# First attention: conditioning two batches ahead, and two products of the adapter merge in its place at the end

## The chip, the cores and the metric

The kernel runs on one core of one Trainium2 chip. The metric is the device time of one execution in microseconds (us). Three runs of the kernel before took 1413.83, 1415.15 and 1416.17 us; their median is 1415.15. All data are float32, but for a small mask in bfloat16.

A core has a matrix engine (TensorE, PE in the profile; PEld is its weight load), a vector engine (VectorE, DVE), a scalar engine for activations and copies (ScalarE, ACT), a general engine (GpSimd, POOL) and a sequencer that issues DMAs (SyncE, SP). Each engine works through its own instructions in order. They wait for one another by semaphores.

## The reference

One transformer block on x of 8 batches x 128 rows x 512 columns.

```python
x = x + attn(cond(x, cond_weight[adapter_ids]), wq, wk, wv, wo)     # first attention
x = x + ffn(cond2(x, Wq, Wk, Wv, Wo, ..., k_cache, v_cache, table, seqlens), ffn weights)

# cond:  h[b] = x[b] @ weight[adapter[b]].T            (512 x 512 per batch, gathered by index)
# attn:  q, k, v = h @ wq, h @ wk, h @ wv              (32 heads of 16, 8 key heads)
#        out = softmax(causal(q k^T * scale)) v @ wo
# cond2: attention with norms, rotary positions and a paged cache (32 heads of 128, 8 key heads)
# ffn:   y @ kernel + bias + low-rank deltas, the low-rank matrices mixed by a gate per batch
```

The change lies in the first attention, which takes the first 212 us or so. The second attention and the feed-forward part fill the rest of the span.

## The kernel before

The text of the program sets the order of every engine's instructions (`manual_schedule`), and the framework adds the semaphores. A tile name with `bufs=n` has n buffers used in turn: the tile after the n-th waits until the first one's readers are done.

**The batch pipeline.** The first attention loops over `k` from 0 to 16. A batch `b` has two rounds, `k = 2b` (even) and `k = 2b + 1` (odd), and each round holds half of its heads. A batch passes through these steps:

- `load_x` (L290): a DMA brings x[b] into `xs_b`, four buffers. The DMAs of batches 2 and 3 are issued by POOL, the others by SP.
- `gather_w` (L296): four indirect DMAs of 256 KB, issued by POOL, bring the batch's 512 x 512 conditioning weight into tiles `cw` from a pool of twelve (tag `a`), which is three batches of weights.
- `flip_x` (L497, L503): PE transposes xs into PSUM and ACT copies it out as `xT` (two buffers).
- `condition` (L512, L520): 16 logical products on PE (32 instructions) give `hp`, which ACT copies out as `hT` (four buffers, tag `vg`).
- `project_k`, `project_v` (L543, L550), `project_q` (L528): the projections of hT. `keep_k`, `keep_v`, `keep_q` copy them out on ACT. `keep_v` also has SP store V to memory (`v_kept`, L572) and load it four times, spread over the partitions (`vrep`, L575).
- `scores1` (L593 mask, L605 products), `max1` on DVE (L616), `exps1` on ACT (L636), `divide1` on DVE and POOL (L644 to L646), `turn1`, DVE's transposes (L655), and `values1` on PE (L671).
- `out_proj1` (L693): PE's product; DVE adds xs (L697) and SP stores the sum (`x_kept`, L698). `flip_x1` (L497, L702) transposes it for the second attention.

In the kernel before, round `2b` makes the conditioning of the next batch, and the key projection that reads it follows on PE a little later in the same round. The lines that set this, as PE meets them in an even round:

```python
scores1(k)                  # of batch b
condition(b + 1)            # products, then ACT copies hT
flip_x1(b - 2)
kv = project_k(b + 1)       # reads that hT
values1(b - 1, (1, 0))
project_v(b + 1, kv)
```

The odd round ends with `project_q(b + 1)`, then `flip_x(b + 2)`, and `load_x(b + 4)` on SP's queue. The tile that this load fills is that of batch `b`, which `out_proj1(b)` reads in round `2b + 3`. SP holds the load until then, and what stands behind it in SP's queue too.

**The merge.** The feed-forward part needs low-rank matrices mixed by the gates. `merge_loads` brings them in, `merge_gates` (L441, L447) prepares gate tiles on DVE and POOL, and `merge_a` (L456, L463) makes one of four products on PE with a copy on ACT. All share the pool of twelve tiles with the conditioning weights. The rounds after the last conditioning also issue the first gathers of the second attention's cache (`vg`, `kg`, L160) on POOL.

**PSUM.** Products of conditioning, projections, out_proj1 and merge_a take turns in two buffers (`p_mm`), transposes and values1 in two others (`p_tp`), scores in two more (`p_sc`).

Of the kernel before, what the change touches and what calls it, by code (L numbers as in the profile page):

```python
# [20 lines left out]
B, S, DM = 8, 128, 512  # L21
# [20 lines left out]
def block_kernel(  # L42
# [47 lines left out]
    def tile_a(shape, name):  # L90
        return both.tile(shape, F32, tag="a", name=name, bufs=12)
# [184 lines left out]
    with (  # L276
# [9 lines left out]
        def load_x(b):  # L286
            if b < B:
                xss[b] = p1.tile([P, DM], F32, tag="xs", name=f"xs_{b}", bufs=4)
                queue = nc.gpsimd if b in (2, 3) else nc.sync
                queue.dma_start(out=xss[b][:], in_=x[b])  # L290

        def gather_w(b):
            if b < B:
                cws[b] = [tile_a([P, DM], f"cw_{b}_{c}") for c in range(KC)]
                for c in range(KC):
                    nc.gpsimd.indirect_dma_start(  # L296
                        out=cws[b][c][:],
                        out_offset=None,
                        in_=cond_w,
                        in_offset=bass.IndirectOffsetOnAxis(ap=idx_w[:, c, b : b + 1], axis=0),  # L300
                    )
# [191 lines left out]
        def transposed(src, name):  # L493

            tp = p_tp.tile([P, 4, P], F32, tag="tp", name=name)
            for c in range(4):
                nc.tensor.transpose(tp[:, c, :], src[:, c * P : (c + 1) * P], ident[:])  # L497
            return tp

        def flip_x(b):  # L500
            tp = transposed(xss[b], f"xTp_{b}")
            xT[b] = both.tile([P, KC, S], F32, tag="kg", name=f"xT_{b}", bufs=2)
            nc.scalar.copy(xT[b][:], tp[:])  # L503

        def condition(b):
            hp = p_mm.tile([P, KC, S], F32, tag="mm", name=f"hp_{b}")
            parts = [(oc, c) for oc in range(KC) for c in range(KC)]
            if b == 0:

                parts.sort(key=lambda part: part[1])  # L510
            for n, (oc, c) in enumerate(parts):
                nc.tensor.matmul(  # L512
                    hp[:, oc, :],
                    cws[b][c][:, oc * P : (oc + 1) * P],
                    xT[b][:, c, :],
                    start=(n == 0 if b == 0 else c == 0),
                    stop=(n == KC * KC - 1 if b == 0 else c == KC - 1),
                )
            hT[b] = both.tile([P, KC, S], F32, tag="vg", name=f"hT_{b}", bufs=4)
            nc.scalar.copy(hT[b][:], hp[:])  # L520

        def new_q(b):
            return p_mm.tile([P, REP, S], F32, tag="mm", name=f"qp1_{b}")
# [24 lines left out]
        def project_v(b, ps):  # L548
            for c in range(KC):
                nc.tensor.matmul(  # L550
                    ps[:, 1, :], hT[b][:, c, :], wv_sb[:, c, :], start=(c == 0), stop=(c == KC - 1)
                )
# [76 lines left out]
        def exps1(k, n):  # L629
            h = H[k]  # L630
            b, hb = divmod(k, 2)
            if hb == 0:
                prs[b, n] = p1.tile([P, 2, 8, S], F32, tag=f"pr1_{n}", name=f"pr1_{b}_{n}")
            sc = h["sc"][n][:].rearrange("p j (h t) -> p (j h) t", t=S)
            for m in range(8):
                nc.scalar.activation(  # L636
                    prs[b, n][:, hb, m, :], sc[:, m, :], AF.Exp, bias=h["nm", n][:, m : m + 1]
                )
# [11 lines left out]
        def turn1(k, n):  # L650


            b, hb = divmod(k, 2)
            pr = prs[b, n][:, hb].rearrange("p m t -> p (m t)")
            nc.vector.transpose(pr, pr)  # L655
# [34 lines left out]
        def out_proj1(b):  # L690
            ps = p_mm.tile([P, DM], F32, tag="mm", name=f"att1_{b}")
            for r in range(REP):
                nc.tensor.matmul(  # L693
                    ps[:], oT[b][:, r, :], wo_sb[:, r, :], start=(r == 0), stop=(r == REP - 1)
                )
            x1[b] = p1.tile([P, DM], F32, tag="x1", name=f"x1_{b}", bufs=1)
            nc.vector.tensor_tensor(x1[b][:], ps[:], xss[b][:], ALU.add)  # L697
            nc.sync.dma_start(out=x1_kept[b][:], in_=x1[b][:])  # L698

        def flip_x1(b):  # L700
            tp = transposed(x1[b], f"x1Tp_{b}")
            nc.scalar.copy(x1T[b][:], tp[:])  # L702
# [17 lines left out]
        for k in range(2 * B + 1):  # L720
            b, hb = divmod(k, 2)
            more, now, last = b + 1 < B, k < 2 * B, k - 1
            if now:
                scores1(k)
            if hb == 0:

                for n in range(2):
                    if k:
                        turn1(last, n)
                    if now:  # L730
                        max1(k, n)
                if more:
                    condition(b + 1)
                if k == 2 * B - 2:
                    for i in range(2):
                        merge_a(i, p_mm.tile([P, 512], F32, tag="mm", name=f"aeff_{i}"))
                if b >= 2:
                    flip_x1(b - 2)
                if now:
                    exps1(k, 0)  # L740
                    exps1(k, 1)
                if more:
                    kv = project_k(b + 1)
                if k == 2 * B:
                    t = p_sc.tile([P, 2, 4 * S], F32, tag="sc", name="merged")
                    for i in range(2):
                        merge_b(i, t[:, i, :])
                    queries(0)
                if k:
                    values1(b - 1, (1, 0))  # L750
                if now:
                    divide1(k, 0)
                if more:
                    project_v(b + 1, kv)
                if k == 2 * B - 2:
                    for i in range(2, KC):
                        merge_a(i, p_mm.tile([P, 512], F32, tag="mm", name=f"aeff_{i}"))
                if k == 2 * B:
                    for i in range(2):
                        merge_w(i)  # L760
                if k:
                    values1(b - 1, (3, 2))
                if now:
                    divide1(k, 1)
                if more:
                    keep_k(b + 1, kv)
                    keep_v(b + 1, kv)

                if b:
                    gather_w(b + 3)  # L770
                if b == B - 3:
                    gather(0, "vg")
                elif b == B - 2:
                    gather(0, "kg")
                if k == 2 * B - 4:
                    merge_gates()
            else:
                max1(k, 0)
                max1(k, 1)
                turn1(last, 0)  # L780
                if b >= 1:
                    out_proj1(b - 1)
                exps1(k, 0)
                exps1(k, 1)
                divide1(k, 0)
                divide1(k, 1)
                turn1(last, 1)
                if more:
                    ps = new_q(b + 1)
                    project_q(b + 1, ps, range(REP - 1))  # L790
                else:
                    for c in range(KC):
                        q_matmul(0, c)
                    for part in q_turn(0):
                        part()
                    for c in range(KC):
                        kv_matmul(0, c)
                if more:
                    project_q(b + 1, ps, (REP - 1,))
                    keep_q(b + 1, ps)  # L800
                else:
                    kv_turn(0)
                    norms(0)
                if b + 2 < B:
                    flip_x(b + 2)
                load_x(b + 4)
                if b == 1:
                    tables(0)
                    load_qkv(0)
                    load_wo(0)  # L810
                elif b == 2:
                    tables(1)
                    nc.gpsimd.memset(minus_half[:], -0.5)
                elif b == 3:
                    load_qkv(1)
                if b == 4:
                    indices()
                    nc.sync.dma_start(out=bias[:], in_=ffn_b.unsqueeze(0).to_broadcast([P, DM]))
                    merge_loads()
# [407 lines left out]
```

## Time and profile before

| | us |
|---|---|
| median of three runs | 1415.15 |
| the profiled execution, whole | 1413.75 |
| its span, first to last instruction | 1412.0 |
| PE busy in the span | 1379.3 (98%) |
| DVE, ACT, POOL busy | 931.5, 649.6, 569.9 |
| a steady batch of the first attention (65.8 to 85.8) | 20.0 |
| PE busy in that stretch | 19.76 |

The profile's page gives the busy time of each engine, the granted clock of PE, and the costliest groups of instructions. Answers from its trace give the same for any stretch: instructions in order of time (start, length, engine, line of the program, output and inputs, shape, count), with the idle time before one of them in square brackets and the engine or DMA that ended it. The waits list who waited for whom: total us, number of times, longest. Times are from the start of the span. SPq marks the issue of a DMA by SP, not its transfer. A DMA's landing shows only where an instruction waits for it.

### The profile page before, as it was taken

The page shows a single profiled execution, that of the slowest core. Times are in us where ns is not written, and L with a number is a line of the kernel's source. Part 1 is how long each engine was busy: PE and PEld are TensorE (multiplying, and loading weights), DVE is VectorE, ACT ScalarE, POOL GpSimd, SP SyncE. Part 2 cuts the span into 40 slices and gives each one's busy share as a digit, 9 for nine tenths or more (in the row PEclk, how much of TensorE's full clock was granted, in tenths as well). Part 3 has the DMA queues.
Part 4 walks back from the last instruction along what each step waited for, and adds up shares of the span by engine and source line. Part 5 has one row for each costly group of instructions (what it writes and reads, how often), then busy time and mean ns, then how long its engine had stood idle before and what let it go on. Part 6 is the DMA issues. An engine that isn't in the chain of part 4 may idle for free.

```text
span 1412.0 us, 21833 instructions
## 1 busy us (share of the span) xinstructions
PE 1379.3 (98%) x7012; PEld 889.7 (63%) x7012; DVE 931.5 (66%) x2251; ACT 649.6 (46%) x1515; POOL 569.9 (40%) x557
## 2 busy tenths in 40 slices
PE   6999999999999999999999999999999999999998
PEld 5777755666666666666666666666666565566555
DVE  3878756666666666666666666666666666666651
ACT  3555525444444444444444444444444344344431
POOL 5685633433333333444444343333343433343220
PEclk9999989999999999999999999999999999999999
DMA  7255503444444765444446654444456544444440
GB/s 247 81 160 168 173 31 102 132 119 118 118 119 118 204 180 121 120 120 120 120 120 192 177 136 120 118 120 120 119 165 191 151 111 132 135 111 110 116 112 31
DMA packets 161970, 185.62 MB, mean 131 GB/s; under 512 B 93057, under 2 KB 103553, under 8 KB 161857
## 3 DMA queue, kind: packets, MB, share of 16 engines
q1 hardware_dynamic: 146304, 139.64, 35.5%
q0 software_dynamic: 15552, 44.58, 11.0%
q8 instruction: 57, 0.93, 0.3%
q14 instruction: 57, 0.46, 0.1%
HBM read 80.03 MB, written 5.77 MB: 61 GB/s over the span
## 4 chain that ended last, share of the span: by engine, by line
PE 92%; DVE 2%; ACT 1%; issue 1%; POOL 1%; DMA 1%; SPq 1%; DVEq 0%; POOLq 0%; ACTq 0%
PE op L988 19%; PE qp L177 15%; PE sc L914 15%; PE yp L1007 15%; PE kvp L217 7%; PE sc L921 4%; PE fp L1069 2%; PE qTp L254 2%; PE hp L512 2%; PE o L671 2%; PE att L693 1%; PE qp L528 1%; PE sc L605 1%; ACT pr L636 1%; DMA cw<-in_cond_w_dram,idx_w 1%
## 5 line engine op out<-in xcount | busy, mean ns | idle before, releaser
L927 DVE CUSTOM_DVE_ANT_0 pr<-sc,mask,nq 128x640 f32<-128x640 f32 x256 | 225.9, 884 | 141.1 <-PE sc L921 129.4
L937 ACT ACTIVATE pr<-pr,nm 128x640 f32<-128x640 f32 x256 | 211.8, 827 | 190.0 <-DVE nm L927 187.2
L914 PE MATMUL sc<-kT,qT 128*128 128x512 f32 x512 | 263.3, 596 | 0.0
L177 PE MATMUL qp<-wq,x1T 128*128 128x512 f32 x512 | 251.2, 593 | 0.0
L988 PE MATMUL op<-pT,vg 128*128 128x256 f32 x1024 | 242.0, 379 | 1.4 <-DMA pT<-fl 1.4
L203 POOL TENSOR_TENSOR qa<-qa,qb 128x512 f32<-128x512 f32 x64 | 81.8, 1278 | 376.6 <-DVE sums L904 376.5
L1007 PE MATMUL yp<-wo,oT 128*128 128x512 f32 x504 | 228.6, 596 | 0.0
L988 PEld LDWEIGHTS op<-pT,vg 128*128 128x128 f32 x1024 | 193.9, 190 | 27.7 <-DVE sums L904 1.6
L905 ACT ACTIVATE pr<-pr,sums 128x640 f32<-128x640 f32 x256 | 208.4, 814 | 0.0
L908 DVE STREAM_TRANSPOSE fl<-pr 128x640 f32<-128x640 f32 x252 | 189.2, 808 | 0.0
L921 PEld LDWEIGHTS sc<-kTo,qT 128*128 128x128 f32 x512 | 96.7, 190 | 125.1 <-issue 103.7
L1007 PEld LDWEIGHTS yp<-wo,oT 128*128 128x128 f32 x504 | 91.4, 191 | 92.5 <-issue 91.1
L160 POOL DMA_INDIRECT kg<-in_k_cache_dram,idx_kv x128 | 132.2, 1033 | 35.3 <-issue 35.2
L160 POOL DMA_INDIRECT vg<-in_v_cache_dram,idx_kv x128 | 127.4, 995 | 37.6 <-issue 32.6
L914 PEld LDWEIGHTS sc<-kT,qT 128*128 128x128 f32 x512 | 88.1, 192 | 81.3 <-issue 78.1
L256 ACT COPY qT<-qTp 128x512 f32<-128x512 f32 x64 | 37.5, 586 | 209.5 <-PE qTp L254 206.1
L217 PEld LDWEIGHTS kvp<-wkv,x1T 128*128 128x128 f32 x512 | 97.3, 190 | 40.5 <-issue 30.4
L217 PE MATMUL kvp<-wkv,x1T 128*128 128x256 f32 x512 | 121.0, 379 | 0.0
L244 POOL TENSOR_TENSOR rs<-ss,minus_half 128x5 f32<-128x5 f32 x64 | 76.5, 1196 | 82.6 <-DVE ss L242 81.7
L177 PEld LDWEIGHTS qp<-wq,x1T 128*128 128x128 f32 x512 | 82.9, 191 | 32.0 <-issue 32.0
L921 PE MATMUL sc<-kTo,qT 128*128 128x128 f32 x512 | 99.4, 276 | 0.0
L273 ACT COPY kTo<-kTp 128x128 f32<-128x128 f32 x64 | 17.1, 267 | 163.6 <-PE kTp L271 163.6
(151 smaller groups left out, 1671.2 us busy)
## 6 DMA issues: line engine op xcount, KB each, us to landing
pT<-fl SPq DMA_DIRECT2D x1008, 80.0 KB
kT<-flk SPq DMA_DIRECT2D x480, 32.0 KB
wq<-in_wq_dram SPq DMA_DIRECT2D x8, 1024.0 KB
wo<-in_wo_dram SPq DMA_DIRECT2D x8, 1024.0 KB
vrep<-v_kept SPq DMA_DIRECT2D x32, 128.0 KB
wkv<-in_wkv_dram SPq DMA_DIRECT2D x8, 512.0 KB
vg<-in_v_cache_dram,idx_kv POOLq DMA_INDIRECT x128, 3.7
kg<-in_k_cache_dram,idx_kv POOLq DMA_INDIRECT x128, 3.8
```

Source lines behind the costliest of these rows:

```text
L160: nc.gpsimd.indirect_dma_start(out=dst[:, c].rearrange("p n d -> p (n d)"), out_offset=None, in_=src, in_offset=bass.IndirectOffsetOnAxis( ...
L177: nc.tensor.matmul(s["qp"][:].rearrange("p h d -> p (h d)"), x1T[b][:, c, :], weights[g][0][:, c, :], start=(c == 0), stop=(c == KC - 1),)
L203: nc.gpsimd.tensor_tensor(qa[:], qa[:], qb[:], ALU.add)
L217: nc.tensor.matmul(s["kp"][:], x1T[b][:, c, :], weights[g][1][:, c, :], start=(c == 0), stop=(c == KC - 1))
L905: nc.scalar.activation(prs[r][:], prs[r][:], AF.Copy, scale=sums[:, r : r + 1])
L908: nc.vector.transpose(s["flips"][:, :, :, r, :].rearrange("p b c j -> p c b j"), prs[r][:])
L914: nc.tensor.matmul(sc[:, : NBLK * P].rearrange("p (k j) -> p k j", j=32), s["qT"][:, r, :], s["kT"], start=True, stop=True,)
L921: nc.tensor.matmul(sc[:, NBLK * P : NK], s["qT"][:, r, :], s["kTo"][:], start=True, stop=True)
L927: nc.vector.tensor_tensor_reduce(out=pr[:], in0=sc[:, :NK], in1=mask[:], scale=s["nq"][:, r : r + 1], scalar=3.0e38, op0=ALU.add, op1=ALU.min,
L937: nc.scalar.activation(pr[:], pr[:], AF.Exp, bias=nm[:, r : r + 1], scale=-1.0, accum_out=sums[:, r : r + 1],)
L988: nc.tensor.matmul(ops[h][:, : 2 * S], cached(u, "vg", c) if c < NBLK else s["vo"][:], s["pT"][:, :, c, 2 * h : 2 * h + 2, :].rearrange("p ...
L1007: nc.tensor.matmul(yp[:], s["oT"][:, r, :], weights[g][2][:, r, :], start=(r == 0), stop=(r == REP - 1))
```

## The change

The conditioning of batch b + 2, rather than b + 1, stands in round 2b. Round 0 keeps condition(1), and makes condition(2) as well, with its flip, after project_v. Round 12 has no conditioning left and takes merge_a(0) and merge_a(1) from round 14. The supply moves with it:

- `flip_x(b + 3)` instead of `flip_x(b + 2)` at the end of an odd round.
- `gather_w(4)` in round 1, and `gather_w(b + 4)` instead of `gather_w(b + 3)` in even rounds.
- `load_x(b + 3)` behind `out_proj1(b - 1)` in odd rounds, instead of `load_x(b + 4)` at their end. The same tiles are loaded in the same order.
- `merge_gates` in round 10 instead of round 12.

No instruction is added or removed. The lines after the edited part move down by up to seven.

```diff
@@ -729,9 +729,11 @@
-                if more:
-                    condition(b + 1)
-                if k == 2 * B - 2:
+                if k == 0:
+                    condition(1)
+                elif b + 2 < B:
+                    condition(b + 2)
+                elif b == B - 2:
                     for i in range(2):
                         merge_a(i, p_mm.tile([P, 512], F32, tag="mm", name=f"aeff_{i}"))
@@ -752,6 +754,9 @@
                 if more:
                     project_v(b + 1, kv)
+                if k == 0:
+                    flip_x(2)
+                    condition(2)
@@ -767,12 +772,12 @@
                 if b:
-                    gather_w(b + 3)
+                    gather_w(b + 4)
                 if b == B - 3:
                     gather(0, "vg")
                 elif b == B - 2:
                     gather(0, "kg")
-                if k == 2 * B - 4:
+                if b == B - 3:
                     merge_gates()
@@ -780,11 +785,14 @@
                 if b >= 1:
                     out_proj1(b - 1)
+                    load_x(b + 3)
                 exps1(k, 0)
                 exps1(k, 1)
                 divide1(k, 0)
                 divide1(k, 1)
                 turn1(last, 1)
+                if b == 0:
+                    gather_w(4)
@@ -801,9 +809,8 @@
-                if b + 2 < B:
-                    flip_x(b + 2)
-                load_x(b + 4)
+                if b + 3 < B:
+                    flip_x(b + 3)
```

## The prediction

> **What bounds the kernel now.** I read the page first, then the waits of TensorE (PE) inside the first attention, then the instructions in order of time around each place that the change touches.
>
> ```profile
> span 1412.0 us, 21833 instructions
> PE 1379.3 (98%) x7012; PEld 889.7 (63%) x7012; DVE 931.5 (66%) x2251; ACT 649.6 (46%) x1515; POOL 569.9 (40%) x557
> ```
>
> PE is busy for 98% of the span, so the change can win only idle PE time, and whatever makes PE wait costs its full length. The first attention is the stretch from 25 to 212 us; a steady batch (two rounds k) takes 20.0 us there. Its PE waits (us in total, times, longest):
>
> ```profile
> PE sc L593 <- ACT pr L636: 3.5, 3, 1.8
> PE kvp L543 <- ACT hT L520: 2.6, 7, 0.7
> PE o L671 <- DVE pr L655: 1.3, 2, 1.1
> ```
>
> The second line is what the change aims at: the key projection stands right behind the conditioning whose copy hT it reads. The first is a hole of 3.3 us in round k=0 (PE, then ScalarE (ACT), in order of time: start, us):
>
> ```profile
> 32.14 1.06 PE L550 MATMUL kvp<-wv_sb,hT 128*128 128x128 f32 x8
> 36.70 0.40 PE L593 MATMUL sc<-eye,causal 32*128 32x128 bf16 x14 [1.84 <-ACT pr L636]
> 44.27 0.40 PE L593 MATMUL sc<-eye,causal 32*128 32x128 bf16 x14 [0.27 <-ACT pr L636]
> ...
> 32.40 4.25 ACT L636 ACTIVATE pr<-sc,nm 128x128 f32<-128x128 f32 x16
> ```
>
> PE waits from 33.2 to 36.7 for the sixteen exponentials, because the next scores need their PSUM banks. The end of one odd round (k=3):
>
> ```profile
> 60.74 0.65 DVE L697 TENSOR_TENSOR x<-att,xs 128x512 f32<-128x512 f32 x1
> 61.42 0.35 SPq L290 DMA_DIRECT2D xs<-in_x_dram  x1
> 61.87 0.38 SPq L572 DMA_DIRECT2D v_kept<-vpad  x1
> 63.85 0.60 PE L497 MATMUL xTp<-ident,xs 128*128 128x128 f32 x4
> 66.77 2.10 SPq L575 DMA_DIRECT2D vrep<-v_kept  x4
> ```
>
> The add (L697, ends 61.39) frees an input tile; the load into it leaves at once. The flip at 63.85 reads a tile loaded much earlier. The store v_kept, issued at 61.87, had landed only at 66.77, when its reader could issue: 4.90 us, with the weight gathers (POOL, 59.64 to 64.38) on the same DMA engines. Batch 3 shows 103.16 to 107.59, 4.43 us.
>
> **The change, part by part** (+ is later; all sums are against the profiled execution, 1413.75 us with 1412.0 of span).
>
> *Waits removed.* From round 2 on, project_k reads an hT made one batch earlier. The wait was 0.66 us in round 2, and 0.24 in rounds 4, 6 and 8: -0.66 and -0.72. In round 10 it was 0.24 and a wait for VectorE (DVE) of 0.21 followed it, set by a chain behind L378; a PE that comes later (below) loses both: -0.45. Round 0 keeps its wait, since condition(1) stays there.
>
> *Round 0: flip_x(2) and condition(2).* PE is given four transposes (0.44 us between starts) and 32 products (3.78) in the hole. But the copy xT that condition(2) reads goes into ACT's queue behind the sixteen exponentials, which end at 36.65. So the transposes run in the hole, condition(2) starts at 37.0, and queued behind it on PE is scores1(1), behind that max, exponentials and scores1(2). Here the clock matters (stretches of time: PE busy, its instructions, granted PE clock, DMA):
>
> ```profile
> 13.30:16.70 3.40, 1.53 (x13) 0.99 0.98 367
> 16.70:20.10 3.40, 3.40 (x17) 0.51 1.03 387
> 33.70:37.10 3.40, 0.63 (x20) 1.00 0.02 5
> 37.10:40.50 3.40, 3.40 (x24) 0.50 0.14 43
> ```
>
> Twice a stretch of 3.4 us with little PE work is followed by 3.4 us at half clock. Before, the second of these slowed scores1(1) by 0.5 us and a projection (L528, 4.71 us instead of 3.73) that waited for ACT anyway. After, the same slow stretch falls on condition(2): 3.78 + 1.7 puts its end at 42.5 and scores1(1)'s (1.47) at 44.0, where it was 38.7: **+5.3**. (At full clock +3.8.) kvp_1 now gives its PSUM buffer to project_q(1), after keep_v(1) behind hT_2 on ACT, about 44.05: nothing to speak of. The gathers for batch 2 have landed by then: the DMA share is 0.02 from 33.7 on.
>
> *The loads of x.* load_x(4..7) moves from behind the flip to behind out_proj1, in the round in which flip_x now reads that very tile; SP issues the x1 store first. From the add's end to the flip are 2.46 us (61.39 to 63.85, the same in every batch). The load takes the place in the queue that v_kept had, 0.48 us after the add. Lands at 0.48 + 4.90 + 0.33 (128 KB more ahead of the landing, an estimate from the 387 GB/s of the stretch above), less 2.46: a stall of 3.25 us in round 3; by batch 3's row 2.8 in round 7; between them 3.0 in round 5. In round 9 no weight gather is left beside it: the quiet v_kept (37.41 to 40.52, 3.11) gives 1.46, and the load res late in the kernel (issued 1231.81, read 1234.76, behind a store too) 0.97; I take 1.2. Sum **+10.25**. Behind the flip on PE stand scores1 of the next round and so everything. From below: 4 x 0.97 = 3.9, if gathers don't hinder; from above: 4 x 4.5 = 18, if the vrep loads and large weight loads, now just ahead and behind on SP, queue in as well. No cover is left, as the flip is among the last products of the round.
>
> The Trainium skill weighs in here ("DMA: Bandwidth & Descriptors", Anatomy of one DMA): about 2.0 us fixed plus bytes over 436 GB/s, for the POOL path, which would be 2.6 us for these 256 KB, a stall of 0.6, 2.5 in all. The rows that share the chip's DMA with gathers say 4.4 to 4.9 for half the bytes; I follow the rows.
>
> *The clock after these stalls.* The skill's rule ("TensorE: Matmul & The Clock Gate", HAM oscillation) is to avoid gaps over about 3.4 us; stalls of 3 us would then be free of it, and this part 0. The row at 13.3 speaks otherwise: 1.53 us of work, a gap of 1.9, and half clock followed, while 30.3 to 33.7 with 2.22 of work stayed full. So a stall near 3 us, however it falls across two such stretches, trips the clock about 8 times in 10. One costs 1.35 us, since half of a slow stretch of 3.4, less what falls on idle time, is lost: 3 x 0.8 x 1.35 = **+3.2**; round 9's stall is too short.
>
> *The other moves on the queues.* gather_w goes one batch ahead by taking its first place in round 1 (POOL is free from about 53 to 59) and leaves round 8; there POOL comes earlier, but DVE is held by L378. load_qkv and load_wo are no longer held behind a waiting load on SP and start some 15 us sooner; nothing waited for them. 0.
>
> *The end.* merge_gates moves from round 12 to round 10, merge_a(0, 1) (3.56 us) from 14 to 12, condition(7) out of 12.
>
> ```profile
> 165.59 0.94 POOL L160 DMA_INDIRECT kg<-in_k_cache_dram,idx_kv  x1 [0.30 <-issue]
> 166.56 2.33 POOL L447 TENSOR_TENSOR gs<-gc,sel 128x256 f32<-128x256 f32 x4
> 168.85 3.74 POOL L646 TENSOR_TENSOR pr<-pr,sums 128x1024 f32<-128x1024 f32 x2
> ...
> 167.96 3.72 PE L456 MATMUL aeff<-gs,la 128*128 128x256 f32 x16
> 174.33 1.07 PE L671 MATMUL o<-pr,vrep 32*32 32x128 f32 x40 [1.12 <-DVE pr L655]
> ```
>
> Here POOL sets the time: gathers, gates (2.33), divisions, then DVE's transposes, then o at 174.33. Without the gates o can start 2.29 earlier: -2.29. merge_a no longer fills the time before; PE idles from 168.4 to 172.0. The gates now stand in round 10 behind the vg gathers (to 146.53) and push round 12's transposes to 154.3, where PE wants o at 153.56: +0.79. Together **-1.5**. The idle 3.6 us also drop the clock: **+1.2**. So PE's total work is unchanged, and the emptied slot at the end pays back 2.3, not 3.6.
>
> **Sum:** 5.3 - 0.66 + 10.25 + 3.2 - 0.72 - 0.45 - 1.5 + 1.2 = +16.6. On its own execution 1413.75 gives 1430.4. The median of the runs shown is 1415.15, 1.4 above it: **1431.8 us**, slower. A change of less than 0.2%, 2.8 us, can't be told from none.
>
> **Rivals.**
> *Short stalls, no clock loss (15%).* The loads land as the quiet rows say and stalls stay near 1.2: 5.3 - 0.66 + 4.8 - 2.67 + 1.2 = +8.0, 1423. For it: DMA share in the stretch is under one half on the mean. Against: v_kept's 4.4 and 4.9.
> *Long stalls (11%).* Each near 4.5 us, four clock drops at 1.5: +5.3 - 0.66 + 18 + 6 - 2.67 + 1.2 = +27, 1442. For it: v_kept took 9.2 us beside large weight loads (124.19 to 133.39). Against: those loads now come after.
> *Loads in time, not slower (6%).* The load lands within 1.98 us of its issue, in rounds 3 to 9, and stalls and their clock losses go: 5.3 - 0.66 - 2.67 = +2.0 without a drop at the end, 1417.2, within 0.2%. It decides once the four stalls together are under 0.8 us. Against: no 256 KB load here was used sooner than 2.95 us.
> *The order doesn't do what it says.* PE still waits for hT where the copy is late: 1.8 us less gain. A share of the cases above, no more.
>
> **How the numbers follow.** The likeliest (68%): stalls of 2.3 to 3.6, +12 to +21. The range takes in the short stalls and the lower part of the long ones: 1421.5 to 1440. Outside: loads in time, and most of the long. Faster 0.03 (loads in time and a shorter half-clock stretch after 204 us, whose phase may move by 1.7 us), same 0.05, slower 0.92.
>
> **What would show it.** Right: four waits of the xTp transposes for the xs load, three near 3 us and a last near 1.2; the kvp wait for hT only in round 0; condition(2) starting at 37 under half clock and scores1(1) ending near 44; an idle PE of about 3.6 us before o in round 14. Wrong: no xTp wait for xs, or one under 1 us each; a full clock after the stalls; condition(2) inside the hole.

## The result, and the profile after

The changed kernel takes 1432.02 us (median of six runs, 1424.87 to 1435.46), the kernel before beside it 1414.49 us (six runs, 1412.11 to 1416.17). The ratio is 1.0109, with a 95% interval of 1.0087 to 1.0132: slower by 1.1%. (The ratios in this document are worked out over all runs of both kernels; the quotient of the two medians is near them, 1.0124 here.) The forecast was 1431.8 us and slower. The profiled execution of the changed kernel took 1432.41 us with a span of 1430.6, so the two traces differ by 18.6 us of span, against +16.6 in the sum. The runs also spread more than before, over 10.6 us instead of 4.1.

The page of the changed kernel, the span and the busy time:

```profile
span 1430.6 us, 21837 instructions
PE 1386.5 (97%) x7012; PEld 894.7 (63%) x7012; DVE 931.1 (65%) x2251; ACT 650.2 (45%) x1515; POOL 570.0 (40%) x557
```

PE has the same 7012 instructions and is busy 7.2 us longer (1379.3 before). So of the 18.6 us, 7.2 are the same work done more slowly, and 11.4 are idle PE. The waits of PE from 25 to 230 us of the changed kernel (us in total, times, longest) say where the idle part is:

```profile
PE xTp L497 <- DMA xs<-in_x_dram: 10.1, 4, 3.7
PE hp L512 <- ACT xT L503: 3.5, 1, 3.5
PE o L671 <- DVE pr L655: 2.2, 2, 1.3
PE sc L605 <- issue: 1.4, 2, 1.0
PE sc L593 <- ACT pr L636: 1.2, 1, 1.2
...
PE kvp L543 <- ACT hT L520: 0.7, 1, 0.7
```

The wait for hT went as intended, from 2.6 us in seven to the 0.7 of round 0. Its place is taken by 10.1 us of the flip's transposes waiting for a load. The hole of round 0 stayed: its wait has a new name (condition(2) for xT) and the same length. PE in order of time (start, us, then the instruction, in brackets the wait before it), round 0 first, then the ends of rounds 3, 5, 7 and 9:

```profile
33.17 0.60 PE L497 MATMUL xTp<-ident,xs 128*128 128x128 f32 x4
37.32 5.47 PE L512 MATMUL hp<-xT,cw 128*128 128x128 f32 x32 [3.54 <-ACT xT L503]
42.72 0.40 PE L593 MATMUL sc<-eye,causal 32*128 32x128 bf16 x16
42.95 1.09 PE L605 MATMUL sc<-kbd,qT 32*128 32x256 f32 x16
...
71.92 0.63 PE L497 MATMUL xTp<-ident,xs 128*128 128x128 f32 x4 [3.48 <-DMA xs<-in_x_dram]
72.48 0.40 PE L593 MATMUL sc<-eye,causal 32*128 32x128 bf16 x16
72.71 1.80 PE L605 MATMUL sc<-kbd,qT 32*128 32x256 f32 x16
74.45 4.74 PE L512 MATMUL hp<-xT,cw 128*128 128x128 f32 x32
...
120.04 0.63 PE L497 MATMUL xTp<-ident,xs 128*128 128x128 f32 x4 [2.29 <-DMA xs<-in_x_dram]
...
144.68 0.63 PE L497 MATMUL xTp<-ident,xs 128*128 128x128 f32 x4 [0.64 <-DMA xs<-in_x_dram]
```

Behind the stall at 71.92 the scores take 1.80 us where they take 1.09 in round 0 of this kernel, and the products of the conditioning 4.74 where 3.84 is their usual length. Stretches like this one make up nearly all of the 7.2 us of slower work: over the first 260 us the granted clock costs 15.3 us in this trace and 8.5 in the one before. The granted clock around three of the stalls (stretch of time: its length, PE busy, clock, DMA share, GB/s):

```profile
69.20:72.60 3.40, 0.68 (x12) 1.00 1.00 354
72.60:76.00 3.40, 3.40 (x39) 0.55 1.06 382
93.00:96.60 3.60, 0.02 (x1) 1.00 0.95 350
96.60:100.00 3.40, 3.31 (x37) 0.53 0.00 0
118.00:120.60 2.60, 0.56 (x5) 1.00 1.02 386
120.60:124.00 3.40, 3.40 (x38) 0.52 1.05 385
```

Each stall is followed by about 3.4 us at half clock, the shortest of the three (2.29 us) too. The fourth column of the stall rows points to why the loads are late: the DMA engines are full (0.95 to 1.02) while PE waits. Whose traffic it is that delays them, a run below tests. One of these loads on SP's queue (start, us):

```profile
65.85 0.34 SPq L698 DMA_DIRECT2D x_kept<-x  x1
66.23 0.43 SPq L290 DMA_DIRECT2D xs<-in_x_dram  x1
66.70 0.48 SPq L130 DMA_DIRECT2D wq<-in_wq_dram  x1
```

Issued at 66.23 and read at 71.92: 5.69 us for 256 KB. POOL issues four gathers of conditioning weights at 64.43, 65.73, 66.98 and 68.23, which move 1 MB at the same time. The load of round 9, which has no such gathers beside it, is read 2.98 us after its issue (141.70 to 144.68).

The starts of the key projection and of the second attention's first scores sum it up:

| | before | after | later by | step |
|---|---|---|---|---|
| project_k, round 2 | 50.34 | 54.88 | 4.5 | 4.5 |
| round 4 | 70.35 | 79.45 | 9.1 | 4.6 |
| round 6 | 90.35 | 104.18 | 13.8 | 4.7 |
| round 8 | 111.64 | 127.58 | 15.9 | 2.1 |
| round 10 | 131.64 | 150.61 | 19.0 | 3.0 |
| round 12 | 152.47 | 169.99 | 17.5 | -1.5 |
| scores, second attention | 211.66 | 229.31 | 17.7 | 0.1 |
| end of the span | 1412.0 | 1430.6 | 18.6 | 0.9 |

### The profile page after: what moved, and what is told of

Read it like the earlier page. It is cut to its first block, busy times and chain, and to the rows that moved or that the text cites. A ratio compares the mean times of both kernels' runs of the same rounds, so it can differ in the third digit from the quotient of the medians.

```text
span 1430.6 us, 21837 instructions
## 1 busy us (share of the span) xinstructions
PE 1386.5 (97%) x7012; PEld 894.7 (63%) x7012; DVE 931.1 (65%) x2251; ACT 650.2 (45%) x1515; POOL 570.0 (40%) x557
## 4 chain that ended last, share of the span: by engine, by line
PE 89%; DVE 3%; DMA 2%; issue 2%; POOL 2%; ACT 1%; SPq 1%; POOLq 0%; DVEq 0%; ACTq 0%
PE op L995 19%; PE qp L177 15%; PE sc L921 15%; PE yp L1014 15%; PE kvp L217 7%; PE sc L928 4%; PE hp L512 2%; PE fp L1076 2%; PE qTp L254 2%; PE o L671 2%; DMA xs<-in_x_dram 1%; PE sc L605 1%; DVE nm L616 1%; ACT pr L636 1%; SPq L968 1%
## 5 line engine op out<-in xcount | busy, mean ns | idle before, releaser
L1014 PEld LDWEIGHTS yp<-wo,oT 128*128 128x128 f32 x504 | 91.4, 191 | 92.6 <-issue 91.2
```

The costliest lines, as they stand in the source:

```text
L1014: nc.tensor.matmul(yp[:], s["oT"][:, r, :], weights[g][2][:, r, :], start=(r == 0), stop=(r == REP - 1))
```

## The experiments

Two theories stood against each other. The first is that of the prediction: the change is slower because the load of x comes too late, made later still by the weight gathers that share the DMA engines, because each stall brings a half-clock stretch, and because condition(2) misses the hole of round 0. The rivals: that the load is late by its queue or its buffer and not by the gathers; that the half clock comes of something else than the stalls; and that the remaining loss lies in the merge at the end.

Runs of one set share a chip and are compared by their ratio to the kernel before in the same set. That kernel took about 1427 us in some sets (1427.17 and 1426.74) and 1413.33 and 1414.79 in others; they are called the 1427 us and the 1414 us sets below. The chip alone doesn't make the difference, as one and the same gave 1427.17 in one set and 1414.79 in another. Where ratios of different sets stand side by side, it is with that reserve.

**The load one round earlier.** The load goes into the even round, into a fifth buffer, and the sum x1 is written over the input tile, so that the memory stays about the same.

```diff
-xss[b] = p1.tile([P, DM], F32, tag="xs", name=f"xs_{b}", bufs=4)
+xss[b] = p1.tile([P, DM], F32, tag="xs", name=f"xs_{b}", bufs=5)
-x1[b] = p1.tile([P, DM], F32, tag="x1", name=f"x1_{b}", bufs=1)
+x1[b] = xss[b]
     flip_x1(b - 2)              # even round
+    if b >= 1:
+        load_x(b + 3)
     out_proj1(b - 1)            # odd round
-    load_x(b + 3)
```

> The changed kernel, but each x tile is loaded one round earlier (even round, fifth buffer; the sum of out_proj1 is written over the x tile to make room). Theory (the flip waits for a load that leaves too late): the four xTp waits, 10.1 us in the changed kernel, and the slow-clock stretches behind the first three, some 4.5 us, both go; what is left is round 0's +5.3 less the waits won: 1416 to 1419 us. Rival (the stall only moves to another wait behind it, such as the weights' gathers or DVE's transposes): a new PE wait of 8 us or more in rounds 4 to 10, 1426 or above.

Measured: 1433.31 us against 1427.17 beside it, a ratio of 1.0028 (1.0005 to 1.0051). No transpose waits for xs any more, and condition(2) still waits 3.5 us for xT. With the load in time, about 0.3% over the kernel before is left, at the upper edge of the forecast (1416 to 1419 us is a ratio of 1.0006 to 1.0027). A new wait stands in this trace, of PE for qT, 9.0 us in five; but the next run, which leaves the conditioning where it was, has 12.4 us of it in six, so it is no sign of the rival.

**The kernel before with the late load alone.** The load goes to where the changed kernel has it; its flip stays one batch later.

```diff
     out_proj1(b - 1)
+    load_x(b + 3)
...
-load_x(b + 4)
```

> The kernel before with only the loads of x moved behind out_proj1, where the changed kernel has them; the flips stay where they were, so each tile is needed a batch later. Theory (the load's place is harmless as long as the flip is not in the same round): no xTp wait, time unchanged within 2 us, 1412 to 1416. Rival (unblocking SP's queue and starting the large weight loads some 15 us sooner is a gain or a loss of its own): 3 us or more away from the kernel before.

Measured: 1427.45 us against 1426.74, a ratio of 1.0012 (1.0001 to 1.0023), and no wait for xs. The new place in SP's queue costs next to nothing while a batch lies between load and flip. So the queue order alone isn't what costs; the flip that now follows it is.

**The hole of round 0.** flip_x(2) goes ahead of condition(1), so that its copy xT stands ahead of the sixteen exponentials in ACT's queue.

```diff
 if k == 0:
+    flip_x(2)
     condition(1)
...
 if k == 0:
-    flip_x(2)
     condition(2)
```

> The changed kernel with flip_x(2) ahead of condition(1), so that the copy xT stands before the exponentials on ACT. Theory (in round 0 condition(2) waits for a copy queued behind sixteen exponentials, and then runs at half clock): condition(2) starts near 33.7 us, the hole is filled, the clock stays full there, scores1(1) ends near 39 instead of 44: 5 us won, about 1427 us. Rival (the hole is needed anyway by the later exponentials, or the weights of batch 2 are not there yet): condition(2) waits for cw, or the gain is eaten by the wait before scores1(2); 1430 to 1432.

Measured: 1434.58 us against 1427.17, a ratio of 1.0051 (1.0029 to 1.0074). The same kernel once more in a 1414 us set:

> The changed kernel with flip_x(2) put ahead of condition(1), once more, for the size of the first part alone. Theory: the changed kernel's 1.2% over the kernel before is made of about 5 us in round 0 and about 12 us of late loads with the clock drops behind them, and the two add up. With round 0 repaired and the loads late as before the ratio is 1.0121 - 5.3/1414 = 1.008 (1.007 to 1.0095), the transposes wait for xs some 10 us in four, and condition(2) runs 3.7 to 3.8 us directly behind project_v. Rival: the parts don't add up, since what PE does in round 0 shifts the later half-clock stretches: then the ratio is nearer to 1.005 or 1.012, with the same waits.

Measured: 1423.56 us (twelve runs), a ratio of 1.0054 (1.0037 to 1.0072), nearly the same as in the 1427 us set. PE in order of time in round 0 of this run:

```profile
32.09 1.06 PE L550 MATMUL kvp<-wv_sb,hT 128*128 128x128 f32 x8
32.98 3.74 PE L512 MATMUL hp<-xT,cw 128*128 128x128 f32 x32
36.65 0.40 PE L593 MATMUL sc<-eye,causal 32*128 32x128 bf16 x16
36.88 1.09 PE L605 MATMUL sc<-kbd,qT 32*128 32x256 f32 x16
```

condition(2) follows the value projection at once, runs at full clock, and ends as the exponentials end; the scores start at 36.88 with no wait, at the very time of the kernel before. The loads are as late as ever: the transposes wait 9.8 us in four. So the queue of ACT, shown here by moving one copy ahead, kept condition(2) out of the hole. Against the changed kernel's 1.0109 or 1.0121 that is 8 or 9 us, with intervals that still allow the forecast's 5.3. The number is the rival's (about 1.005); the theory that the parts simply add up gave 1.008 and was missed, if narrowly. One reason is in the trace: this run lost nothing to the clock from 26 to 50 us, where the changed kernel lost 1.7 us in its first trace and 3.4 in that of its 1414 us set.

**The gathers out of the load's way.** gather_w(b + 4) goes from the even round to the odd one, behind the divisions on POOL.

```diff
-if b:                           # even round
-    gather_w(b + 4)
...
-if b == 0:                      # odd round, behind the divisions
-    gather_w(4)
+gather_w(b + 4)
```

> The changed kernel with gather_w(b + 4) of batches 1 to 3 moved from the even to the odd round, behind POOL's divisions, so that it starts after the x load. Theory (the load is slow because the weight gathers are on the DMA engines): waits of xTp for xs near 1.0 to 1.5 us each instead of 3.5, 3.7 and 2.3, without slow clock behind them: 8 to 9 us won, about 1423. Rival (the chain of x1 store, load and the vrep loads just ahead of it sets the landing): waits stay at 2.5 to 3.5 us, 1430 or above.

Measured: 1443.87 us against 1427.17, a ratio of 1.0095 (1.0059 to 1.0132). The waits for xs went to 2.6 us in four, 0.6 to 0.7 each, and nothing clear was won: in this execution PE waited about 1 us three times for x1T (2.5 in all) and 6.6 us for qT, and long half-clock stretches followed. So this set doesn't tell whether the gathers cost the time. In a 1414 us set it stood beside the changed kernel and a kernel before of 1413.33 us.

> The changed kernel itself, beside the kernel before, on the chip of the runs that follow. Theory: some 15 us above the kernel before (ratio 1.009 to 1.012), with three xTp waits of 2 to 4.5 us and a fourth under 1.3, and slow clock behind the first three. Rival (the loss was that of one chip): ratio under 1.005.

Measured: the changed kernel, no edit, 1430.13 us (four runs), a ratio of 1.0121 (1.0095 to 1.0148), with waits for xs of 9.9 us in four and a half clock behind the first three.

> The changed kernel with the gathers behind the x load, now beside the changed kernel on one chip. Theory: xTp waits of 0.6 to 0.8 us each; where the gathers do no harm in their new place, 8 us below the changed kernel. Rival (the gathers now hold up something else, seen as waits of o for ACT's x1T of about 1 us and slow clock behind them): no gain on the changed kernel, within 3 us of it.

Measured: 1417.95 us (thirteen runs, 1415.35 to 1419.37), a ratio of 1.0030 (1.0018 to 1.0041), 12 us less than the changed kernel on the same chip. Waits of PE from 25 to 230 us in this run, and then the load in round 3 and the transposes that read it:

```profile
PE o L671 <- DVE pr L655: 3.3, 3, 1.7
PE xTp L497 <- DMA xs<-in_x_dram: 2.7, 4, 0.9
```

```profile
65.59 0.43 SPq L290 DMA_DIRECT2D xs<-in_x_dram  x1
66.06 0.46 SPq L130 DMA_DIRECT2D wq<-in_wq_dram  x1
```

```profile
68.68 0.63 PE L497 MATMUL xTp<-ident,xs 128*128 128x128 f32 x4 [0.89 <-DMA xs<-in_x_dram]
70.49 3.84 PE L512 MATMUL hp<-xT,cw 128*128 128x128 f32 x32
```

3.09 us from issue to use instead of 5.69, with the same store ahead of the load on SP and the same large weight load right behind it; only the gathers are elsewhere (70.58 on, behind a load that has landed). That shows that the gathers made this load 2.6 us longer, and rules out the weight load behind it on SP as the cause. The rest of the stall, 0.9 us, is left by the late issue, which needs the buffer that out_proj1 frees; the run with a fifth buffer has no such wait. With the stalls at 0.9 us and less, the conditioning behind them runs at its 3.84 us: no half clock in rounds 3 to 9.

**The clock alone.** Here PE does redundant work in place of the stalls: project_q of the next batch is computed a second time at the end of rounds 3 and 5, and half of it in round 7: some 8.9 us of products whose results are overwritten or thrown away. If the half clock comes of idle PE, it must go, though the loads stay late.

```diff
 # end of the odd round, ahead of flip_x(b + 3)
+if 1 <= b <= 3:
+    project_q(b + 1, ps, range(REP if b < 3 else REP // 2))
```

> The changed kernel with extra, redundant query products on PE in rounds 3, 5 and 7 (four, four and two of the heads made twice into the same place), which stand where PE waits for the x load. Theory (idle PE time of 2 to 4 us drops the clock, at a price of 1.5 us each): the load lands when it did, the xTp waits shrink to about nothing, the clock stays full behind them, about 4.5 us won: 1427 to 1428. Rival ([...]the light products of scores1 behind it drop the clock): slow stretches stay, 1431 to 1433. If the load is what PE itself drives, the extra work adds its 9 us: 1441.

Measured: 1437.26 us against 1427.17, a ratio of 1.0081 (1.0032 to 1.0130), too wide to tell. Once more, in the set of the last two runs:

> The changed kernel with the redundant query products in rounds 3, 5 and 7, now beside the changed kernel on one chip. Theory (an idle PE of 2 to 4 us costs its clock as well): 3 to 5 us below the changed kernel, though PE does 9 us more work. Rival (the clock loss has another source): within 1 us of it, or above.

Measured: 1430.58 us (five runs, 1426.28 to 1434.47), a ratio of 1.0124 (1.0096 to 1.0151), the same as the changed kernel's 1.0121: the rival's number. The trace says both were half right. PE in round 5, and the stretches around it:

```profile
95.98 0.60 PE L497 MATMUL xTp<-ident,xs 128*128 128x128 f32 x4
96.51 0.40 PE L593 MATMUL sc<-eye,causal 32*128 32x128 bf16 x16
96.89 1.15 PE L605 MATMUL sc<-kbd,qT 32*128 32x256 f32 x16
97.96 3.84 PE L512 MATMUL hp<-xT,cw 128*128 128x128 f32 x32
```

```profile
92.00:96.00 4.00, 4.00 (x39) 1.00 0.79 292
96.00:100.00 4.00, 4.00 (x56) 1.00 0.00 0
```

The clock stays at 1.00 behind rounds 3, 5 and 7, where it fell in the changed kernel, so a busy PE in place of the stall does keep it. From the start of condition(2) to project_k of round 8 this kernel takes 86.6 us (37.44 to 124.05), the changed kernel of the same set 91.4 (36.67 to 128.07): 4.8 us less, though PE was given nearly as much work (8.9 us) as the first three stalls had been long (9.5). Between 50 and 150 us the clock cost the changed kernel 5.1 us, and this one nothing. Afterwards it was lost again: one wait of PE, named "issue", 1.78 us long at 151.39, and a half clock behind it and once more near 186 to 193. Why that wait came there was not found out.

**Both repairs, and the merge.** The earlier load and the earlier flip together:

> Both repairs together: x loaded one round earlier, and flip_x(2) ahead of condition(1). Theory (late load and round 0 are all that the change costs): +0.2 in round 0, the hT waits won (-1.8), the end -1.5 and its clock drop +1.2: 1411 to 1413.5 us, at or just below the kernel before. Rival (the pipeline two batches ahead has a further cost of its own, by longer lives of tiles or other queues): 1416 or above.

Measured: 1424.75 us against 1426.74, a ratio of 0.9988 (0.9978 to 0.9998). With the merge's two products and the gates put back where the kernel before has them:

```diff
-elif b == B - 2:                # even round: merge_a(0), merge_a(1)
+elif b == B - 1:
-if b == B - 3:                  # merge_gates
+if b == B - 2:
```

> Both repairs, with the merge as in the kernel before: merge_gates in round 12, merge_a(0, 1) in round 14. Theory (moving the merge wins the gates' 2.3 us in round 14 but loses 0.8 in round 12 and a clock drop of 1.2 to 1.7): within 1.5 us of the run with both repairs and the moved merge; no slow clock in round 14, a PE wait of about 2 us in round 12. Rival (the emptied slot at the end is the gain of the change): 2 us or more slower than that run.

Measured: 1424.74 us, a ratio of 0.9982 (0.9972 to 0.9993). In this set the place of the merge makes no difference that can be measured, as forecast. The forecast wait of about 2 us in round 12 didn't show, though: in both traces PE waits 1.9 us for qT just ahead of it (up to 158.67 and 159.19), a wait that would cover one for the divisions. Last, the same with the first gather of kg moved from round 12 to round 11, out of the way of the divisions:

```diff
-elif b == B - 2:                # even round
-    gather(0, "kg")
+elif b == B - 3:                # odd round, behind the divisions
+    gather(0, "kg")
```

> Both repairs, the merge as in the kernel before, and the kg gather of the second attention moved from round 12 to round 11, where POOL is idle for 4.9 us. Theory (round 14 waits because POOL's gathers and gates stand ahead of its divisions): the wait of o for DVE in round 14 goes, 1.2 us more than without that move; ratio to the kernel before 0.996 to 0.998. Rival (POOL has no slack there either): a new wait in round 12, ratio 0.998 to 1.

Measured: 1411.83 us (fourteen runs) against 1413.33, a ratio of 0.9986 (0.9969 to 1.0003). Waits of o in this run, PE in order of time (the earlier of the two is round 12):

```profile
146.34 1.07 PE L671 MATMUL o<-pr,vrep 32*32 32x128 f32 x40 [1.74 <-DVE pr L655]
...
170.33 1.09 PE L671 MATMUL o<-pr,vrep 32*32 32x128 f32 x46 [0.34 <-ACT x1T L702]
```

The wait for the divisions in round 14 is gone, and one of 1.74 us stands in round 12, with 10.2 us at half clock behind it (from 147.33). The divisions that it waits for (140.84 to 144.59) stand behind the gathers of vg on POOL (136.08 to 140.83) and ahead of those of kg (144.75 on). So it isn't the moved gather that makes this wait. It is the one forecast for the run before: round 12 has neither conditioning nor merge left to fill it. The ratio is the rival's number, and what the moved gather gains by itself was not measured.

## Why the prediction was right

*Size and sign.* 1431.8 us was forecast, 1432.02 measured; the sum of +16.6 met a difference of 18.6 between the two traces. The terms below are measured in those two traces. That the medians meet within 0.2 us is luck: the six runs spread over 10.6 us. In the steps of the table, too, errors cancel: the terms give 3.6 us for round 8 and 1.0 for round 10, measured were 2.1 and 3.0. Waits of PE named "issue", 1.02 us each and foreseen by no term, stand in the kernel before ahead of round 8 and in the changed kernel ahead of round 10.

*Waits removed.* As forecast: the hT wait is left in round 0 alone.

*Round 0, +5.3.* Right in this trace: condition(2) starts at 37.32 (37.0), ends at 42.79 (42.5), scores1(1) end at 43.97 (44.0), where they ended at 38.7. The reason held: moving the copy ahead in ACT's queue closed the hole. The forecast clock drop fell upon condition(2), but its phase isn't fixed: in the changed kernel's trace in the 1414 us set, and in that with redundant work, it covered 36 to 43 us, two stretches instead of one, and condition(2) took 6.4 to 6.7 us.

*The loads, +10.25.* The sum was right, 10.1 us; the single terms less so: 3.48, 3.67, 2.29 and 0.64 for 3.25, 3.0, 2.8 and 1.2. The estimate that took the durations of the rows with gathers beside them is the right one: the run without the gathers gives 3.09 us for the load and 2.7 for the four stalls. That is close to the estimate of 2.5 us for the stalls from the Trainium skill's price of a DMA ("DMA: Bandwidth & Descriptors", Anatomy of one DMA), though the load itself takes 3.09 us where the price says 2.6: the price nearly held once the gathers were gone, and the rows beside gathers held with them.

*The clock, +3.2.* Mis-sized: the step took 8 in 10 of 1.35 us each. All three long stalls lowered the clock, and each took 1.7 us: 5.1. A stretch is lost in full, since little of it fell on idle time. The chance was well judged: in the three traces of the table below that have late loads (9.8 to 10.1 us of stalls) the clock fell behind eight of the nine long stalls. The Trainium skill's rule to avoid idle gaps over about 3.4 us ("TensorE: Matmul & The Clock Gate", HAM oscillation) doesn't go far enough here, as the clock fell behind a stall of 2.29 us too; the prediction did right to follow the row at 13.3.

*The end, -1.5 and +1.2.* o in round 12 waits 0.96 (+0.79 forecast). From there to o in round 14 the changed kernel wins 2.3 us (-2.29). The clock falls behind it, and merge_a takes 5.41 us instead of 3.72, +1.7 for +1.2. One sign did not come, the idle 3.6 us before o in round 14: PE waits only 0.15 and 1.29 us there. That sign didn't agree with the prediction's own terms: with merge_a gone and o 2.29 us earlier, they leave 1.12 + 3.56 - 2.29 = 2.4 us; one more microsecond went in round 13, where the products of the scores (L605) take 2.1 us instead of 1.0, 0.37 of it a wait "issue".

```profile
172.36 1.07 PE L671 MATMUL o<-pr,vrep 32*32 32x128 f32 x40 [0.96 <-DVE pr L655]
...
190.83 1.07 PE L671 MATMUL o<-pr,vrep 32*32 32x128 f32 x40 [1.29 <-DVE pr L655]
191.83 5.41 PE L456 MATMUL aeff<-gs,la 128*128 128x256 f32 x16
197.16 2.01 PE L671 MATMUL o<-pr,vrep 32*32 32x128 f32 x112
```

*Not foreseen.* A wait "issue" of 1.02 us at 134 and a half-clock stretch behind it; the kernel before has such a wait too (an o at 96.33, L671), without the stretch.

*What the change would have been worth.* Adding the granted clock's losses (1 minus the clock, over the first 260 us) and the stalls for xs puts the kernels of about 1414 us side by side:

| | clock lost, us | stalls for xs, us | span, us |
|---|---|---|---|
| before | 8.5 | 0 | 1412.0 |
| changed | 15.3 | 10.1 | 1430.6 |
| changed, 1414 us set | 18.7 | 9.9 | 1427.9 |
| redundant work (8.9 us) | 13.6 | 1.0 | 1427.2 |
| gathers moved | 10.2 | 2.7 | 1415.7 |
| flip ahead | 13.6 | 9.8 | 1423.1 |
| load, flip, merge and kg | 11.9 | 0 | 1409.5 |

The kernel before's span plus what the two columns add to it (and the redundant work) comes near to each: 1428.9 for 1430.6, 1432.1 for 1427.9, 1427.0 for 1427.2, 1416.4 for 1415.7. For the two kernels with the flip ahead it is too long, 1426.9 for 1423.1 and 1415.4 for 1409.5. These 4 and 6 us are what a filled hole and the removed hT waits would give, though one of the others is off by as much. In the last kernel, half of it goes to 3.4 us more of lost clock. That is argued from single traces; what was measured is a version with both repairs 0.1 to 0.2% below the kernel before. Where the half-clock stretches fall differs from run to run; the last section says what the traces show of it.

## What to carry to other kernels

Making a result earlier moves the need for all its inputs as well: before the step is moved, take the time from the issue of each load to its landing in the traffic of its new place, not in quiet, since here 256 KB took 5.7 us beside gathers and 3.1 without. Where PE is the bound, a stall of two or three us is to be counted with half of a 3.4 us stretch on top (eight times in nine here). A filler for a hole has to have its own inputs made before the thing that makes the hole: one copy standing behind sixteen exponentials kept 3.5 us of idle PE open.

## What was not expected of the hardware

The length of a stall doesn't settle whether the clock falls. It fell behind stalls of 1.98 and 2.29 us for xs (the changed kernel's two traces), and stayed full behind one of 2.07 in the run with the flip ahead; it fell behind "issue" waits of 0.71 us (flip ahead) and 1.02 (changed kernel), and stayed full behind one of 1.02 in the kernel before. The traces settle more than that. In each of them the half-clock stretches keep a beat of 3.413 us: in the changed kernel's they start at 38.81, 72.94, 96.84, 120.73 and 134.38 us, which is 10, 7, 7 and 4 beats apart, and last one beat or a few. The beat lies differently in each execution, and so catches a stall or splits it. The stall of 2.29 us left PE busy for 33% of one beat (117.32 to 120.73), that of 1.98 us for 42%; the one of 2.07 us was split over two beats, 80% and 59% busy.

Busy time alone doesn't explain the rest: before the second attention of the kernel before, PE is busy for all of a beat (200.97 to 204.38), and three beats at half clock follow. But that beat holds nothing but products of o (L671, 1.57 us) and of the merge's weff (L482, 1.98). If the time of these two kinds is counted at 0.4 and that of all others in full, one limit fits the seven traces of the table: from 20 to 300 us, 508 beats at full clock, the 29 with a sum below 0.49 of the beat were followed by half clock, and no other was. The "issue" waits fit too: 0.40 and 0.45 where the clock fell, 0.58 in the kernel before. Weight and limit are an estimate, fitted to these traces. Applied unchanged to the seven traces of the 1427 us sets they miss 2 of 488 beats, both in the run with the merge put back. Why these products count for less is not shown. The differing beat would also help to explain the spread of 10.6 us, but that is only argued.

The kernel before took about 1427 us in some sets and 1413 to 1415 in others. In the 1427 us sets each trace has the copy qT on ACT, at 25 to 31 us, start after a wait of 2.9 to 5.7 us, put down to "remote". In the kernel before with the load moved it reads:

```profile
29.73 0.60 ACT L538 ACTIVATE qT<-qp 128x512 f32<-128x512 f32 x1 [5.29 <-remote]
```

In the first trace of the kernel before this copy starts at 24.90 after 0.27 us, for PE. PE then waits for qT 12.4 us in six, and 0.8 in two there. What makes the difference was not found; it is why the comparisons go by ratios within one set.
